# The norm of the group after next starts one front earlier: an SSM mixer stack on one core

## The chip, the cores and the metric

The kernel runs on one core of a Trainium2 chip. The metric is the device time of one execution in microseconds, over several runs. Everything is computed in float32 (a few masks and sums in 16 bits), from inputs in HBM to an output in HBM.

## The reference, cut to what matters

The input is x, four sequences of 1024 tokens with 512 features. Four layers run one after the other: a Mamba-2 mixer A, a gated feed-forward, a second mixer B, and the same kind of feed-forward again; each adds to the stream of tokens. A mixer is, cut to its core:

```
h    = layernorm(x)
z, hBC, dt = split(h @ in_proj)              # 1024, 1024 + 2*N, heads
hBC  = silu(causal_conv1d(hBC, taps=4))      # each channel by itself
h, B, C = split(hBC)
dt   = softplus(dt + dt_bias);  a = -exp(A_log) * dt
# in chunks: inside of a chunk and through a state S of each head
L    = exp(segment_sum(a))                   # lower triangle, per head
y    = ((C B^T) * L) @ (dt * h)  +  exp(cumsum a) * (C S)  +  D * h
S    = exp(sum a) * S + B^T (decay * dt * h)
y    = gated rms norm of y and silu(z)       # A: gate, then norm; B: norm, then gate
x    = x + y @ out_proj
```

Mixer A has 16 heads of 64 channels and a state of 64, mixer B 64 heads of 16 channels and a state of 128. A feed-forward normalizes x, forms a gate from a 512 x 512 product, an aggregate with a 512-2048-512 network of one token per sequence, and a last norm.

## The kernel before, in words

**Tiles and stages.** The 4096 tokens are 32 tiles of 128. The stream x goes through HBM between the layers: each layer loads its tiles and stores them again. Mixer A takes the time from 0 to about 1145 us, the first feed-forward to about 1340, mixer B to about 2815, the last feed-forward to the end. The first feed-forward leaves its last twelve tiles unfinished; their last steps (`last_step`, L1367 to L1384: adds on POOL, a norm and two products on VectorE) run inside the norm of mixer B's groups.

**A mixer's groups.** A mixer works in 16 groups of two chunks (`GC = 2`), a chunk being one tile; four groups make a sequence. `Group` loads the two x tiles of a group (from the pool `xp`) on SP's queue. Three things happen to a group, in three different iterations of the main loop (L1005 to L1028). In iteration n, the chunks of group n run (`chunk`, L763 to L976). Between their yields the *front* of group n+1 is emitted piece by piece (`front`, L443 to L629). Inside that front the *norm* of group n+2 is emitted, again piece by piece (`norm`, L389 to L441).

**The norm** has three parts. *Measure*: statistics of both tiles on VectorE (L396 to L398) and a reciprocal root on POOL (L223). *Scaling*: one small VectorE operation for each tile (L417) and one ScalarE operation (L419) that writes the normalized tile xn. *Turning*: eight 128 x 128 transposes on TensorE (L434) into the tile xnT, with a ScalarE copy from PSUM for each token tile (L436); the first three columns of xnT are the previous group's last tokens, copied by POOL (L429). A group with unfinished tiles has its last steps ahead of measure, and measures each tile as soon as it is finished. The norm is a generator: without steps, its first `next` emits measure, the third the scaling, the sixth hands the transposes over; with steps the work is spread over nine.

**The front** has 18 pieces (17 in A): a *gate* piece is one 128-column part of the z product and, for every second, its tanh and the VectorE product L541; a *conv* piece is one product of in_proj (L347), the first tap on ScalarE (L470), three more on VectorE (L474), and the silu of the piece before (L481 to L494). The products for dt (L503, read on VectorE at L511) are small ones. The softplus of dt (from L548) is emitted beside the pieces from the seventh on.

**The order.** TensorE, VectorE, ScalarE and POOL execute exactly in the order of emission (`manual_schedule`); only SP's order (loads and small stores) is laid by the scheduler. Small products (dt, transposes, the sums of the next chunk: `prologue`) stand in a list `small`; each large product pops one after itself (L346), and `finish` empties what is needed at a chunk's beginning. A chunk yields an estimate of the time for which it would leave TensorE waiting; the main loop emits pieces of the front, at 1.75 or 1.9 us each, until that is used up. When the pieces are exhausted, the loop stops there and what is left in `small` goes at the next `finish`.

**A chunk of mixer B** has four quarters of the heads: `decays` forms the exponents of L in PSUM, ScalarE takes exp (L806), VectorE multiplies by C B^T (`weigh`, L813), and TensorE multiplies with the values (`inner`, L829) into py; `close_y` (L878 to L885), `to_state` (L909), and the tail of the chunk (`tail`: the output product L670, the sum of squares ssq L672, the update of x L686, its statistics L229) follow, the tail inside the next chunk. Mixer A has one quarter in each chunk.

**The last steps' buffers.** xp has six x tiles, xnT three buffers. A feed-forward loads its even tiles to five tiles of its own pool, its odd ones to six of xp.

Of the kernel before, what the change touches and what calls it, by code (L numbers as in the profile page):

```python
# [8 lines left out]
F32 = mybir.dt.float32  # L9
# [6 lines left out]
P = 128  # L16
GC = 2
GT = GC * P
D = 512
KD = D // P  # L20
# [5 lines left out]
HIST = TAPS - 1  # L26
# [46 lines left out]
def hybrid_kernel(  # L73
# [40 lines left out]
    NT = NB * NCH  # L114

    const = ctx.enter_context(tc.tile_pool(name="const", bufs=1))
    xp = ctx.enter_context(tc.tile_pool(name="xp", bufs=6, reuse_waits="tile"))
    dr = ctx.enter_context(tc.tile_pool(name="dr", bufs=1, space=bass.MemoryType.DRAM))
    wts = ctx.enter_context(tc.tile_pool(name="wts", bufs=1))

# [100 lines left out]
    def rsqrt(v):  # L221

        nc.gpsimd.tensor_tensor(v, v, neg_half[: v.shape[0]], ALU.pow)  # L223
# [23 lines left out]
    def mixer(m, in_w, conv_w, conv_b, dt_bias, A_log, Dv, norm_w, out_w, src, dst, first, stats, last_steps={}):  # L247
# [18 lines left out]
        with stack:  # L266
            wk = stack.enter_context(tc.tile_pool(name=f"wk_{m.name}", bufs=1, reuse_waits="tile"))
# [5 lines left out]
            def mm(name):  # L273
                return p_mm.tile([P, 512], F32, tag="mm", name=name)
# [69 lines left out]
            small = []  # L344
# [13 lines left out]
            def defer(part, steps, first=False):  # L358

                runs = []  # L360
                for n, step in enumerate(steps):
                    last = n == len(steps) - 1
                    if last:
                        pending.append((part, None))

                    def run(step=step, last=last):
                        step()
                        if last:
                            pending[:] = [p for p in pending if p[0] is not part]

                    runs.append(run)
                small[:] = runs + small if first else small + runs
# [16 lines left out]
            def norm(f, prev):  # L389

                tag = f.tag
                mv = sm.tile([P, GC, 3], F32, tag="mv_x", name=f"mv_{tag}")

                def measure(c):
                    st = sm.tile([P, 6], F32, tag="st_x", name=f"st_{tag}_{c}")
                    nc.vector.bn_stats(st, f.xs[c])  # L396
                    nc.vector.bn_aggr(mv[:, c, 0:2], st)
                    nc.vector.tensor_scalar_add(mv[:, c, 1:2], mv[:, c, 1:2], 1e-5)  # L398
                    rsqrt(mv[:, c, 1:2])

                if f.steps:

                    for n in range(6):
                        for c in reversed(range(GC)):
                            if 0 <= n - 2 * c < 4:
                                next(f.steps[c])
                            if n - 2 * c == 3:
                                measure(c)
                        yield
                else:  # L410
                    for c in range(GC):
                        measure(c)
                    yield
                    yield
                xns = []
                for c in range(GC):
                    nc.vector.scalar_tensor_tensor(mv[:, c, 2:3], mv[:, c, 0:1], -1.0, mv[:, c, 1:2], ALU.mult, ALU.mult)  # L417
                    xn = wk.tile([P, D], F32, tag="xn", name=f"xn_{tag}_{c}", bufs=2)
                    nc.scalar.activation(xn, f.xs[c], AF.Identity, bias=mv[:, c, 2:3], scale=mv[:, c, 1:2])  # L419
                    xns.append(xn)  # L420
                yield
                yield
                if not f.steps:
                    yield
                xnT = f.xnT = wk.tile([P, KD, HIST + GT], F32, tag="xnT", name=f"xnT_{tag}", bufs=3)
                if prev is None:
                    nc.gpsimd.memset(xnT[:, :, 0:HIST], 0.0)
                else:
                    nc.gpsimd.tensor_copy(xnT[:, :, 0:HIST], prev.xnT[:, :, GT : GT + HIST])  # L429

                def turn(c, k, tps={}):
                    if k == 0:
                        tps[c] = mm(f"tpx_{tag}_{c}")
                    nc.tensor.transpose(tps[c][:, k * P : (k + 1) * P], xns[c][:, k * P : (k + 1) * P], ident)  # L434
                    if k == KD - 1:
                        nc.scalar.copy(  # L436
                            xnT[:, :, HIST + c * P : HIST + (c + 1) * P], tps[c].rearrange("p (k t) -> p k t", k=KD)
                        )

                defer(xnT, [lambda c=c, k=k: turn(c, k) for c in range(GC) for k in range(KD)])  # L440
                yield  # L441

            def front(f, behind):  # L443
# [5 lines left out]
                tag = f.tag  # L449
                xnT = f.xnT  # L450
# [159 lines left out]
                more = norm(behind, f if behind.b == f.b else None) if behind is not None else iter(())  # L610
                soft = softplus()
                for at, (kind, n) in enumerate(steps):
                    if kind == "gate":
                        if n == 7:
                            defer(f, prologue(f, 0))
                        gate(n)
                        if n == 6:
                            silu(order[-1])
                    else:
                        convolve(order[n])  # L620
                        if n > 0:
                            silu(order[n - 1])

                    if at >= (2 if behind is not None and behind.steps else 4):
                        next(more, None)
                    if at >= 6:
                        next(soft, None)
                    yield 1.75 if kind == "gate" else 1.9
# [352 lines left out]
            with tc.manual_schedule(  # L981
                engines={
                    mybir.EngineType.PE,
                    mybir.EngineType.DVE,
                    mybir.EngineType.Activation,
                    mybir.EngineType.Pool,
                }
            ):
                fs = [Group(*groups[0]), Group(*groups[1])]
                for _ in norm(fs[0], None):  # L990
                    pass
                if first:
                    lay_constants()
                    lay_flags(range(TS))
                weighing = weigh_rows()
                for at, _ in enumerate(front(fs[0], fs[1])):
                    catch_up()
                    if at >= 6:
                        next(weighing, None)
                for _ in weighing:  # L1000
                    pass
                lay_sums(fs[0], 0)
                if first:
                    lay_flags(range(TS, SETS))
                for n in range(len(groups)):  # L1005
                    if n + 2 < len(groups):
                        fs.append(Group(*groups[n + 2]))
                    f, ahead, behind = (fs + [None, None])[n : n + 3]
                    pieces = front(ahead, behind) if ahead is not None else iter(())
                    due = 0.0  # L1010
                    for c in range(GC):
                        following = (f, c + 1) if c + 1 < GC else (None if ahead is None else (ahead, 0))
                        for us in chunk(f, c, following):
                            due += us
                            while due > 0.0:
                                waiting, later_on[:] = later_on[:], []
                                piece = next(pieces, None)
                                for step in waiting:
                                    step()
                                if piece is None:  # L1020
                                    break
                                due -= piece
                            catch_up()
                    for _ in pieces:
                        catch_up()
                state.pop("fold")()
                for _ in state["tail"]:
                    catch_up()  # L1028
# [3 lines left out]
    def ffn(r, src, dst, stats, filling, bias_on_pe):  # L1032
# [10 lines left out]
        with stack:  # L1043
            wk = stack.enter_context(tc.tile_pool(name=f"wk_f{r}", bufs=1, reuse_waits="tile"))
# [4 lines left out]
            p_c = stack.enter_context(tc.tile_pool(name=f"c_f{r}", bufs=2, space=PSUM))  # L1049

            def load_tile(i, name):
                pool, n = ((wk, 5), (xp, 6))[i % 2]
                t = pool.tile([P, D], F32, tag="x", name=name, bufs=n)
                nc.sync.dma_start(t, src[i])
                return t
# [94 lines left out]
            for s in range(4):  # L1150
                tag = f"{r}_{s}"
# [60 lines left out]
            for i in filling[: len(filling) - last]:  # L1212
                tag = f"{r}_{i}"
# [129 lines left out]
            behind = [] if leaves else [(i, True) for i in filling]  # L1343
# [123 lines left out]
```

## Time and profile before

| | us |
|---|---|
| median of 3 runs | 3059.65 |
| the 3 runs | 3053.1 to 3065.45 |
| profiled execution, its own time | 3044.65 |
| its span (first to last instruction) | 3042.9 |
| TensorE busy in the span | 2767.9 |
| VectorE busy | 2081.7 |
| ScalarE busy | 1261.8 |
| POOL busy | 720.3 |
| mean granted TensorE clock | 0.963 |

The profile is one execution, taken on the core. Its first page gives busy time by engine, then the costliest groups of instructions by line. Behind it the trace can be asked for the waits of each engine (which instruction waited for which, the total, how often, and the longest), for a table of busy time by stretches, and for the order of time of all instructions in a stretch, with the idle time of the engine before each and what ended it. Names have a letter for the layer: _a, _b for the mixers, _f for a feed-forward. PE is TensorE, PEld its weight loads, DVE VectorE, ACT ScalarE, POOL GpSimd, SP the engine whose queue issues the loads.

### The profile page before, as it was taken

Reading aid. Unit: us, or ns where it says so; the run is one execution under the profiler, and the core shown is the slowest. Engines: PE = TensorE matmul, PEld = TensorE weight load, DVE = VectorE, ACT = ScalarE, POOL = GpSimd, SP = SyncE. Lnnn points to the kernel's source line nnn. Section 1 sums busy time; section 2 is a strip of 40 time slices with the busy share of each in tenths; the row PEclk is TensorE's granted clock in tenths of the full one; section 3 lists DMA queues with packets and bytes.
Section 4 is the critical chain, followed back from the end, with each engine's and each line's share of the span. In section 5 each row is a group of like instructions: output and inputs, shape, how many; then the busy total and the mean of one; then the engine's idle time right before and its main releaser. Section 6 shows DMA issues by size and latency. Waiting matters only on the chain. (4 is left out here: it accounts for less than half of the span.)

```text
span 3042.9 us, 46127 instructions
## 1 busy us (share of the span) xinstructions
PE 2767.9 (91%) x17156; PEld 1789.5 (59%) x17156; DVE 2081.7 (68%) x4417; ACT 1261.8 (41%) x2874; POOL 720.3 (24%) x839
## 2 busy tenths in 40 slices
PE   7999999999999988999999899999888888898986
PEld 5666666666666653456666666666555565564332
DVE  5667666766666662477777687776787777875368
ACT  3334433334333332355444444444444444443245
POOL 1222122122212221351111112212222222212057
PEclk8999999999999999999999999999999999998999
DMA  3000000000000015430000000000000000001423
GB/s 117 14 19 16 16 16 17 24 17 17 16 17 22 10 68 205 154 102 10 17 20 20 13 20 18 13 17 21 22 25 21 20 23 20 13 11 72 170 88 110
DMA packets 92959, 124.25 MB, mean 41 GB/s; under 512 B 38728, under 2 KB 42328, under 8 KB 92736
## 3 DMA queue, kind: packets, MB, share of 16 engines
q1 hardware_dynamic: 80960, 98.23, 10.0%
q10 hardware_dynamic: 9792, 16.82, 1.5%
q0 software_dynamic: 1984, 6.26, 0.6%
q8 instruction: 136, 2.23, 0.3%
q14 instruction: 87, 0.71, 0.1%
HBM read 84.54 MB, written 36.72 MB: 40 GB/s over the span
## 5 line engine op out<-in xcount | busy, mean ns | idle before, releaser
L347 PE MATMUL pc_b<-xnT_b,w_in_b 128*128 128x259 f32 x1280 | 355.7, 408 | 25.1 <-DVE S_b L909 21.9
L813 DVE TENSOR_TENSOR L_b<-L_b,Gm_b 128x1024 f32<-128x1024 f32 x256 | 308.7, 1247 | 2.9 <-ACT L_b L806 2.9
L347 PE MATMUL pz_a<-xnT_a,w_in_a 128*128 128x256 f32 x1024 | 296.5, 408 | 2.9 <-ACT Bt_a L756 2.3
L347 PE MATMUL pc_a<-xnT_a,w_in_a 128*128 128x259 f32 x1152 | 299.1, 394 | 0.0
L806 ACT ACTIVATE L_b<-seg_b 128x512 f32<-128x512 f32 x512 | 263.6, 603 | 74.0 <-PE seg_b L799 74.0
L347 PE MATMUL pz_b<-xnT_b,w_in_b 128*128 128x256 f32 x1024 | 291.4, 397 | 2.9 <-ACT xnT_b L436 2.9
L474 DVE SCALAR_TENSOR_TENSOR u_b<-pc_b,cw_b,u_b 128x256 f32<-128x256 f32 x480 | 231.5, 482 | 79.8 <-ACT u_b L470 68.3
L347 PEld LDWEIGHTS pc_b<-xnT_b,w_in_b 128*128 128x128 f32 x1280 | 229.3, 198 | 92.7 <-DVE S_b L909 25.4
L474 DVE SCALAR_TENSOR_TENSOR u_a<-pc_a,cw_a,u_a 128x256 f32<-128x256 f32 x432 | 208.2, 482 | 73.6 <-ACT u_a L470 63.3
L1205 PE MATMUL g_ps<-gw,xnT_f 128*128 128x512 f32 x512 | 246.9, 619 | 9.6 <-DMA gw<-in_L_ffn_gate_w 4.2
L829 PE MATMUL py_b<-L_b,hdt_b 128*32 128x128 f32 x4096 | 165.7, 299 | 97.6 <-DVE L_b L813 96.5
L670 PE MATMUL pout_a<-w_out_a,h_a 128*128 128x512 f32 x512 | 240.2, 613 | 0.0
L670 PE MATMUL pout_b<-w_out_b,h_b 128*128 128x512 f32 x512 | 235.7, 604 | 0.0
L347 PEld LDWEIGHTS pc_a<-xnT_a,w_in_a 128*128 128x128 f32 x1152 | 200.9, 190 | 58.5 <-DVE rs_a L685 11.4
L882 POOL TENSOR_TENSOR h_b<-h_b,z_b 128x256 f32<-128x256 f32 x128 | 90.8, 730 | 509.5 <-ACT sq_b L881 509.5
L347 PEld LDWEIGHTS pz_a<-xnT_a,w_in_a 128*128 128x128 f32 x1024 | 172.3, 195 | 55.0 <-ACT out_a L679 14.4
L347 PEld LDWEIGHTS pz_b<-xnT_b,w_in_b 128*128 128x128 f32 x1024 | 174.5, 194 | 48.8 <-issue 26.0
L829 PEld LDWEIGHTS py_b<-L_b,hdt_b 128*32 128x32 f32 x4096 | 112.6, 117 | 147.7 <-DVE L_b L813 60.5
L1205 PEld LDWEIGHTS g_ps<-gw,xnT_f 128*128 128x128 f32 x512 | 93.2, 196 | 122.1 <-issue 113.5
L881 ACT ACTIVATE sq_b<-h_b 128x256 f32<-128x256 f32 x128 | 47.9, 417 | 262.5 <-DVE h_b L878 262.5
L670 PEld LDWEIGHTS pout_a<-w_out_a,h_a 128*128 128x128 f32 x512 | 93.3, 192 | 100.1 <-issue 96.3
L670 PEld LDWEIGHTS pout_b<-w_out_b,h_b 128*128 128x128 f32 x512 | 92.3, 190 | 99.5 <-issue 95.7
(321 smaller groups left out, 4919.7 us busy)
## 6 DMA issues: line engine op xcount, KB each, us to landing
d<-in_L_ffn_d_w SPq DMA_DIRECT2D x4, 2048.0 KB
x_f<-xa SPq DMA_DIRECT2D x32, 256.0 KB
xb<-x_b ACTq DMA_DIRECT2D x32, 256.0 KB
x_f<-xb SPq DMA_DIRECT2D x32, 256.0 KB
x_a<-in_L_attn_a_x SPq DMA_DIRECT2D x30, 256.0 KB
xa<-x_a ACTq DMA_DIRECT2D x30, 256.0 KB
out<-x_f SPq DMA_DIRECT2D x22, 256.0 KB
xf<-x_f SPq DMA_DIRECT2D x20, 256.0 KB
```

Source lines behind the costliest of these rows:

```text
L347: nc.tensor.matmul(*args, **kw)
L474: nc.vector.scalar_tensor_tensor(u, ps[:, k : k + GT], cw[:, j, k : k + 1], u, ALU.mult, ALU.add)
L670: nc.tensor.matmul(pout, f.hs[e // 2][:, e % 2, cols], w_out[:, e, :], **on)
L806: nc.scalar.activation(L[:, r], sg[r0 + r], AF.Exp)
L813: nc.vector.tensor_mul(Lr, Lr, Gm.unsqueeze(1).to_broadcast([P, 2 * HB, P]))
L829: nc.tensor.matmul(py[cg * CT : (cg + 1) * CT, e % 4, :], hdt[:, h // HC, u : u + HC, :], Ls[half][:, r, hq, :], start=not started[cg], st ...
L881: nc.scalar.activation(sr, yh, AF.Square)
L882: nc.gpsimd.tensor_mul(yh, yh, zs[half * 2 + r][:, :, cols])
L1205: nc.tensor.matmul(ps, xnT[:, k, :], gw[:, k, :], start=(k == 0), stop=(k == KD - 1 and not bias_on_pe))
```

## The change

Four things are changed.

1. In `front`, the norm of the next group but one takes its step ahead of a piece's products instead of behind them, and begins at the first piece instead of the fifth (the third, where the group has unfinished tiles). Without steps, measure is emitted ahead of gate 0 instead of behind gate 2, the scaling ahead of conv 0 instead of behind conv 2, and the transposes are handed over ahead of gate 3 instead of behind gate 4.
2. The pool of x tiles has eight buffers instead of six, the pool of turned tokens xnT two instead of three.
3. Where no pieces are left, the main loop emits one small product for each 0.35 us of the estimate instead of stopping.
4. A feed-forward's even tiles have four buffers of its own pool, its odd tiles the eight of xp.

```diff
-    xp = ctx.enter_context(tc.tile_pool(name="xp", bufs=6, reuse_waits="tile"))
+    xp = ctx.enter_context(tc.tile_pool(name="xp", bufs=8, reuse_waits="tile"))
...
-                xnT = f.xnT = wk.tile([P, KD, HIST + GT], F32, tag="xnT", name=f"xnT_{tag}", bufs=3)
+                xnT = f.xnT = wk.tile([P, KD, HIST + GT], F32, tag="xnT", name=f"xnT_{tag}", bufs=2)
...
                 for at, (kind, n) in enumerate(steps):
+
+                    next(more, None)
                     if kind == "gate":
...
                             silu(order[n - 1])
-
-                    if at >= (2 if behind is not None and behind.steps else 4):
-                        next(more, None)
                     if at >= 6:
                         next(soft, None)
...
                                 if piece is None:
+
+                                    if small:
+                                        small.pop(0)()
+                                        due -= 0.35
+                                        continue
                                     break
...
-                pool, n = ((wk, 5), (xp, 6))[i % 2]
+                pool, n = ((wk, 4), (xp, 8))[i % 2]
```

## The prediction

> **What bounds the kernel now.** I read the busy totals, then the waits by engine, then busy time by stage, then the timeline of single groups. Rows give start, duration, engine, line, operation; brackets give the idle time before it and its cause.
>
> ```profile
> PE 2767.9 (91%) x17156; PEld 1789.5 (59%) x17156; DVE 2081.7 (68%) x4417; ACT 1261.8 (41%) x2874; POOL 720.3 (24%) x839
> ...
> PE py_b L829 <- DVE L_b L813: 96.5, 71, 5.8
> PE tpg L1193 <- ACT xn_f L1186: 34.9, 12, 3.2
> PE ssq_a L672 <- DVE sq_a L972: 28.8, 14, 2.7
> PE pc_b L347 <- DVE S_b L909: 21.9, 12, 2.2
> ```
>
> TensorE does 2767.9 us of a 3042.9 us span, so the time is its work plus its waits. The largest are in mixer B, where py (L829) waits for VectorE's weighing L813: 96.5 us in 71 waits. Few of these are spare capacity: TensorE's order is written by hand, and what stands behind a waiting matmul waits too. The stages:
>
> ```profile
> 100.00:1100.00 1000.00, 962.15 (x5162) 653.13 (x5161) 677.14 (x1603) 382.65 (x955) 209.64 (x277) 0.98 0.06 17
> 1470.00:2030.00 560.00, 521.66 (x3954) 355.62 (x3955) 409.02 (x793) 250.77 (x585) 101.58 (x115) 0.98 0.06 18
> 2080.00:2650.00 570.00, 501.36 (x3717) 338.63 (x3715) 440.11 (x835) 249.09 (x571) 148.31 (x146) 0.95 0.07 20
> 2910.00:3030.00 120.00, 91.47 (x260) 43.30 (x258) 98.81 (x197) 66.79 (x110) 90.00 (x90) 0.96 0.34 114
> ```
>
> Columns: window, its length, busy PE, PEld, DVE, ACT, POOL, granted clock, DMA share, GB/s. Mixer A (row 1) is bound by TensorE, 96% busy. Mixer B without unfinished tiles (row 2) is at 93%; its groups that also finish tiles of the first feed-forward (row 3) at 88%, with DVE and POOL busier. The last feed-forward (row 4) is VectorE's.
>
> **Moving the norm.** It removes and adds no engine instruction in a steady group: bn_stats and its two followers (L396 to L398) twice, L417 twice, two ACT scalings (L419), eight transposes, two ACT copies only change places. Here is what they stand in front of, from one group of mixer B without steps:
>
> ```profile
> 1570.10 0.22 DVE L511 TENSOR_TENSOR v_b<-pd_b,dtb_b 128x64 f32<-128x64 f32 x1 [1.88 <-PE pd_b L503]
> ...
> 1572.72 0.22 DVE L511 TENSOR_TENSOR v_b<-pd_b,dtb_b 128x64 f32<-128x64 f32 x1 [2.33 <-PE pd_b L503]
> ...
> 1576.22 0.56 ACT L470 ACTIVATE u_b<-pc_b,cb_b,cw_b 128x256 f32<-128x256 f32 x1 [0.50 <-PE pc_b L347]
> ...
> 1578.12 1.51 DVE L474 SCALAR_TENSOR_TENSOR u_b<-pc_b,cw_b,u_b 128x256 f32<-128x256 f32 x3
> ...
> 1579.61 2.35 DVE L813 TENSOR_TENSOR L_b<-L_b,Gm_b 128x1024 f32<-128x1024 f32 x2
> ...
> 1582.02 0.65 PE L829 MATMUL py_b<-L_b,hdt_b 128*32 128x128 f32 x16 [0.37 <-DVE L_b L813]
> ...
> 1589.75 0.68 DVE L396 BATCH_NORM_STATS2 st_b<-x_b 128x6 f32<-128x512 f32 x1
> ...
> 1595.92 0.82 ACT L419 ACTIVATE xn_b<-x_b,mv_b 128x512 f32<-128x512 f32 x1 [1.69 <-DVE mv_b L417]
> ```
>
> *Measure.* It takes VectorE from 1589.75 to 1591.75, 2.0 us. Its new place is ahead of the first L511, where VectorE idles 1.88 and 2.33 us for TensorE: hidden, 0. At the old place nothing is gained: afterwards VectorE waits 0.94 us more for ACT's u (L470), which waits for products, before L813 of the last heads can come.
>
> *Scaling.* In the new order, L417 stands on VectorE after both first L813, rs, the x update and its statistics, just ahead of L474 at 1578.12; the two L419 stand on ACT directly ahead of the u (L470) that L474 reads, which was done at 1576.78. So u now waits for L417, which is ready at about 1578.2: two scalings at a pitch of 0.72 plus L470 at about 0.6 end near 1580.3. Add the semaphore and L474 starts near 1580.4, where it started at 1578.12: a VectorE bubble of about 2.2 us. Behind it stand L691 and the L813 that py at 1582.02 waits for already (0.37 us). Nothing is left to hide it, so TensorE stops 2.2 us longer. ACT's next four exponentials, behind u too, end near 1582.5 instead of 1580.8, ahead of their L813 at 1585. In the old order the same bubble was 1.69 us of ACT, ahead of nothing urgent.
>
> *Transposes.* Eight of 0.27 us, about 0.11 us each beyond what overlaps, 0.9 us, go from the second chunk to the first. In the second chunk TensorE has a 2.03 us wait for S (L909), which is VectorE's, and only grows by what is taken away. Their ACT copy (pitch 0.47) now stands ahead of a u in the first chunk: +0.48, less 0.14 for the L417 that left, +0.3; the order of the rest gives −0.2. Per group 2.2 + 0.3 − 0.2 = 2.3 to 2.4. Bounds: 1.5 if L417 is ready sooner, 3.5 if the copy is waited for in full. Eight groups: **+19** (12 to 28).
>
> *The clock.* A rule to weigh:
>
> ```profile
> 1543.00:1546.50 3.50, 1.47 (x10) 1.24 (x7) 3.46 (x7) 2.33 (x6) 1.42 (x2) 1.00 0.11 28
> 1546.50:1550.00 3.50, 3.50 (x39) 2.61 (x38) 2.50 (x7) 2.05 (x6) 0.00 (x0) 0.51 0.10 24
> ```
>
> One wait of 2.03 us lies in the first row; in the next 3.5 us the granted clock is 0.51. The Trainium skill ("TensorE: Matmul & The Clock Gate", section "HAM oscillation") sets the limit at idle gaps above about 3.4 us; by it a 2.2 us bubble costs 2.2. By the row it can cost another half of 3.4 us, 1.7. The row decides that it can happen; how often, no row says: I take three groups in ten, 8 × 0.3 × 1.7 = **+4** (0 to +14).
>
> **Groups with steps (six, mixer B).**
>
> ```profile
> 2302.94 3.43 DVE L813 TENSOR_TENSOR L_b<-L_b,Gm_b 128x1024 f32<-128x1024 f32 x2
> ...
> 2317.19 1.59 DVE L1384 SCALAR_TENSOR_TENSOR x_b<-sgl,mv_o,x_b 128x512 f32<-128x512 f32 x1
> ...
> 2323.66 2.35 DVE L813 TENSOR_TENSOR L_b<-L_b,Gm_b 128x1024 f32<-128x1024 f32 x2
> ```
>
> Their norm starts two pieces earlier. Now one tile's tail (L1383, L1384 and L396 to L398, 0.74 + 0.75 + 1.0 beside nothing on POOL, about 2.6 us with the pitch; 1.59 instead of 0.75 where POOL works) runs after the last L813 of the chunk (2323.66, for which TensorE waits 5.3 us); after the change both tiles' tails stand in front of it: +2.6. The xn bubble adds up to 2.1 to the first chunk. POOL's adds (1.8 to 2.2 us) fall beside earlier L813, where two took 3.43 instead of 2.35. The work earlier in VectorE's idle gives back 0.3 to 1.7 at ssq. I take +4.5 of 0 to 6: **+27** (0 to 36).
>
> **Mixer A.** There ssq's wait for L972 (2.2 us a group) sits where measure was behind; it vanishes, but the same scaling bubble, 2.2, lands on h (L878) and the next open of py: net 0, **−2** in all for the first group of each batch (range −10 to +10).
>
> **Starts.** In the first front, measure of the second group stood behind enough work that it waited only 9.0 us for x:
>
> ```profile
> 36.89 0.69 DVE L396 BATCH_NORM_STATS2 st_a<-x_a 128x6 f32<-128x512 f32 x1 [9.03 <-DMA x_a<-in_L_attn_a_x]
> ```
>
> It now stands ahead of v, z and every u of that front, and x still lands at 36.9, as other loads fill the queue until then. VectorE then runs from 44 to 60 almost without idle, so most of what waits is lost: **+5** (3 to 8). In mixer B x is there early, and TensorE waits 2.83 us at 1377.7 for the softplus chain (L579), in which measure stands now: **−2**.
>
> **Ends.** In the last group of each mixer no pieces remain, and 13 small products (about 2 us) move from the start of the second chunk into its predecessor's waits: **−4.5** for both (0 to −6). Elsewhere pieces run out only at a chunk's last yield: 0.
>
> **Buffers.** x with eight tiles lets each load start one group earlier at the same place of SP's queue; mixers show only one x wait worth naming, the one above: 0. xnT with two: the third was written after the first's last reader in order, no wait. The feed-forward's even tiles get four buffers, its odd ones eight. A tile is released about eight turns (31 us) after it is loaded, so some loads start late: **+1** (0 to +6); behind them on SP stand the other tile loads, and whoever normalizes them.
>
> **The sum:** 19 + 4 + 27 − 2 + 5 − 2 − 4.5 + 1 = **+47.5** on the profiled execution, 3044.65 (span 3042.9 and 1.75 around it), so 3092. The median of the three runs is 3059.65, 15 higher; I add the difference there: **3107**.
>
> **Rivals.**
> 1. *Faster: the two us of measure were what the weighing waited for.* If L417 is ready before the chunk's first L813 in practice, no bubble comes, and VectorE reaches the last L813 of each chunk 0 up to 2.3 us earlier: 8 × 2.3 + half of ssq_a's 28.8 + 6 × 1 + 4.5, less 5 at the start, is about −38: 3021. For it: the 96.5 us row. Against: ACT's order and the 0.94 us wait. It decides on whether u (L470) of the first convolution waits for L417: if not, this wins.
> 2. *The bubble moves, the total doesn't.* TensorE makes the 2.2 us up at the later wait of 2.31 us for the last L813 (1597.6), as that L813 waited on VectorE's backlog alone: +19 and +4 vanish, step groups come to 0: 5 − 2 − 2 − 4.5 + 1 = −2.5: 3057. Against: everything behind on TensorE, the products that feed the later u among it, shifts alike.
> 3. *Step groups even out:* their early work fits VectorE's idle, +27 becomes 0: 3080.
> 4. *The x loads of the feed-forward stall:* every even tile of 32 late by 1 us: +16 on top, 3123.
>
> **How the numbers follow.** Main 0.5, step groups even 0.22, stalls 0.08, the neutral one 0.08, faster 0.12. The bound for a difference is 0.5%, 15.3 us, about what a measurement of this kernel can tell: below 3044.4 is faster, to 3074.9 the same. Faster 0.12, same 0.08, slower 0.80. The likeliest's own range is 3075 to 3135; with the neutral one below and stalls above, 3050 to 3140.
>
> **What would show it.** Right: ACT's L419 in mixer B starting with an idle before it ended by L417 and followed by L470, L474 with an idle near 2.2 us ended by ACT's u in the first chunk; py's wait for L813 up from 96.5 to about 130; ssq_a's gone, py_a's (L860, on h) up; x_a's wait at the start above 9 us and at an earlier place. Group period in B 88.6 to 91, with steps 95 to 99. Wrong: those waits absent, or the last L813's wait shrunk by as much.

## The result

The changed kernel takes 3083.6 us (median of four runs, 3081.53 to 3090.09); the kernel before, 3056.38 us in its four. The ratio is 1.0088, with a 95% interval from 1.006 to 1.0117: slower, by 18 to 36 us. The forecast was 3107 with a range of 3050 to 3140, slower at 0.80. The direction and the range held; the loss is a little over half of the +47.5 that was summed. The profiled execution has a span of 3079.6 us, 36.7 above the one of before. One of the four runs of a kernel below (every step behind the products, the first front in the old order) took 3727.06 us at a granted clock of 0.685 and is left out of its figures.

**The totals and the waits.** First the busy line of the changed kernel's page, then TensorE's waits (total us, times, longest).

```profile
PE 2775.0 (90%) x17156; PEld 1793.8 (58%) x17156; DVE 2067.0 (67%) x4417; ACT 1262.8 (41%) x2874; POOL 709.6 (23%) x839
```

```profile
PE py_b L828 <- DVE L_b L812: 104.9, 87, 4.5
PE tpg L1197 <- ACT xn_f L1190: 35.2, 13, 3.2
PE py_a L859 <- DVE h_a L877: 34.0, 27, 4.6
PE pc_b L347 <- DVE S_b L908: 26.5, 12, 2.2
...
PE seg_b L788 <- DVE S_b L908: 8.4, 8, 2.3
PE tph_b L708 <- ACT L_b L805: 7.4, 7, 1.4
```

(The lines of the file have moved by one to four: L812 is the weighing that was L813, L877 was L878.) The wait of ssq for the sum of squares in mixer A, 28.8 us before, is gone from the list. In its place stand py_a for h (15.8 before, 34.0 now), more of py_b, and two waits of mixer B that were small before: for S at seg (the product that forms the exponents of L) and for ACT at tph (the transposes of h).

By stage (window, length, busy PE, PEld, DVE, ACT, POOL, granted clock, DMA share, GB/s), with windows moved along where the stage moved:

```profile
100.00:1100.00 1000.00, 967.33 (x5217) 660.16 (x5216) 677.97 (x1623) 392.05 (x980) 212.94 (x278) 0.99 0.06 17
1470.00:2030.00 560.00, 504.25 (x3814) 341.72 (x3813) 393.78 (x777) 240.29 (x561) 99.46 (x115) 0.98 0.06 17
2130.00:2700.00 570.00, 494.57 (x3619) 332.95 (x3620) 425.64 (x813) 239.06 (x548) 130.16 (x140) 0.93 0.06 19
2950.00:3070.00 120.00, 90.03 (x248) 42.16 (x248) 100.95 (x202) 67.30 (x111) 92.81 (x92) 0.94 0.34 110
```

In the same 1000 us of mixer A TensorE now gets through 5217 matmuls where it did 5162; in the 560 us of mixer B without steps, 3814 instead of 3954; with steps, 3619 in 570 us instead of 3717, at a clock of 0.93 instead of 0.95.

**Where the time went.** I cut both profiled executions at the first output product (L670) of each chunk. "Start" ends at the first of these; "steps" are the six groups of mixer B that finish tiles.

| stage | before, us | changed kernel |
|---|---|---|
| start | 94.0 | +9.0 |
| mixer A | 1051.2 | −19.0 |
| feed-forward 0 and start of mixer B | 282.1 | +3.0 |
| mixer B, eight groups without steps | 716.0 | +25.9 |
| mixer B, six groups with steps | 564.1 | +18.4 |
| last group of B | 98.4 | −2.0 |
| feed-forward 1 | 237.2 | +1.5 |

Two opposite effects are in the sum: mixer A is faster and mixer B slower, though the same code moves in both. The column is a difference of two single profiles; what it becomes over several is said behind the experiments.

**The place of the scaling.** The timeline of the changed kernel in a group's first chunk of mixer B, VectorE, ACT and TensorE in turn:

```profile
1481.96 0.22 DVE L417 SCALAR_TENSOR_TENSOR mv_b<-mv_b 128x1 f32<-128x1 f32 x2
1484.21 1.52 DVE L474 SCALAR_TENSOR_TENSOR u_b<-pc_b,cw_b,u_b 128x256 f32<-128x256 f32 x3 [2.03 <-ACT u_b L470]
...
1482.21 0.81 ACT L419 ACTIVATE xn_b<-x_b,mv_b 128x512 f32<-128x512 f32 x1 [2.65 <-DVE mv_b L417]
...
1482.93 0.80 ACT L419 ACTIVATE xn_b<-x_b,mv_b 128x512 f32<-128x512 f32 x1
1483.63 0.55 ACT L470 ACTIVATE u_b<-pc_b,cb_b,cw_b 128x256 f32<-128x256 f32 x1
...
1479.37 0.66 PE L347 MATMUL pc_b<-xnT_b,w_in_b 128*128 128x259 f32 x2
...
1484.71 0.33 PE L708 MATMUL tph_b<-ident,h_b 128*128 128x128 f32 x1 [1.00 <-ACT L_b L805]
...
1486.99 0.64 PE L828 MATMUL py_b<-L_b,hdt_b 128*32 128x128 f32 x16 [0.85 <-DVE L_b L812]
1488.13 0.65 PE L828 MATMUL py_b<-L_b,hdt_b 128*32 128x128 f32 x16 [0.49 <-DVE L_b L812]
...
1504.30 0.65 PE L828 MATMUL py_b<-L_b,hdt_b 128*32 128x128 f32 x16 [1.80 <-DVE L_b L812]
```

ACT stands idle 2.65 us for L417, although the product that u reads is finished (its last matmuls, L347, end at 1480.03). The two scalings and u follow, and VectorE waits 2.03 us for that u: the step that the prediction put at 2.2. TensorE pays 1.00 + 0.85 + 0.49 us where it paid 0.37. At the chunk's last weighing it gets 0.5 us back: 1.80 us, where it waited 2.31:

```profile
1509.30 0.64 PE L829 MATMUL py_b<-L_b,hdt_b 128*32 128x128 f32 x16 [2.31 <-DVE L_b L813]
```

(This line is the kernel before, in the same group.)

**Idle and clock together.** The trace also has the stretches of half clock. For the chunks of each kind I took their length, TensorE's idle (gaps over 0.15 us) and the time at half clock, all means in us. "First" and "second" are a group's two chunks, and in brackets stands how many were taken. Half of the half-clock time is lost, if TensorE has work: in the profile of before, successive products of mixer B at L347 start 221 ns apart at the full clock and 432 ns apart at the half one (medians).

| chunks | before: length, idle, half clock | changed | all steps behind the products (below) |
|---|---|---|---|
| A, first (13) | 33.73, 0.09, 0.00 | 36.70, 1.83, 0.79 | 35.16, 0.66, 0.00 |
| A, second (13) | 35.86, 2.63, 2.10 | 31.66, 0.48, 0.00 | 31.64, 0.48, 0.00 |
| B, first (8) | 46.55, 3.88, 2.56 | 50.76, 5.58, 5.12 | 47.29, 3.91, 1.28 |
| B, second (8) | 42.94, 3.02, 3.41 | 41.97, 4.21, 0.85 | 42.15, 4.12, 1.28 |
| B with steps, first (6) | 50.96, 6.23, 7.40 | 54.53, 8.54, 7.96 | 51.01, 5.84, 6.26 |
| B with steps, second (6) | 43.06, 4.12, 1.14 | 42.55, 3.43, 3.41 | 42.76, 3.59, 2.28 |

In a first chunk of B, +4.21 is 1.70 of idle, 1.28 of clock (half of 5.12 − 2.56) and a rest of 1.23, which I take for the transposes' work. In its second chunk 0.88 of work and 1.28 of clock go away, and 1.19 of idle comes.

### The profile page after: what moved, and what is told of

It is laid out like the page before. It is cut to its first block, busy times and chain, and to the rows that moved or that the text cites. A ratio compares the mean times of both kernels' runs of the same rounds, so it can differ in the third digit from the quotient of the medians.

```text
span 3079.6 us, 46072 instructions
## 1 busy us (share of the span) xinstructions
PE 2775.0 (90%) x17156; PEld 1793.8 (58%) x17156; DVE 2067.0 (67%) x4417; ACT 1262.8 (41%) x2874; POOL 709.6 (23%) x839
## 3 DMA queue, kind: packets, MB, share of 16 engines
q0 software_dynamic: 1984, 6.26, 0.6%
## 5 line engine op out<-in xcount | busy, mean ns | idle before, releaser
L347 PE MATMUL pc_b<-xnT_b,w_in_b 128*128 128x259 f32 x1280 | 366.6, 418 | 39.2 <-DVE S_b L908 26.5
L474 DVE SCALAR_TENSOR_TENSOR u_b<-pc_b,cw_b,u_b 128x256 f32<-128x256 f32 x480 | 231.7, 483 | 149.4 <-ACT u_b L470 138.0
L812 DVE TENSOR_TENSOR L_b<-L_b,Gm_b 128x1024 f32<-128x1024 f32 x256 | 308.4, 1246 | 2.8 <-ACT L_b L805 2.8
L347 PE MATMUL pc_a<-xnT_a,w_in_a 128*128 128x259 f32 x1152 | 306.2, 398 | 0.0
L347 PEld LDWEIGHTS pc_b<-xnT_b,w_in_b 128*128 128x128 f32 x1280 | 236.5, 203 | 109.8 <-DVE S_b L908 30.1
L347 PE MATMUL pz_a<-xnT_a,w_in_a 128*128 128x256 f32 x1024 | 295.3, 408 | 2.6 <-ACT Bt_a L755 1.9
L347 PE MATMUL pz_b<-xnT_b,w_in_b 128*128 128x256 f32 x1024 | 293.7, 398 | 3.1 <-ACT xnT_b L436 3.1
L474 DVE SCALAR_TENSOR_TENSOR u_a<-pc_a,cw_a,u_a 128x256 f32<-128x256 f32 x432 | 208.3, 482 | 91.8 <-ACT u_a L470 81.4
L828 PE MATMUL py_b<-L_b,hdt_b 128*32 128x128 f32 x4096 | 162.4, 292 | 106.1 <-DVE L_b L812 104.9
L347 PEld LDWEIGHTS pc_a<-xnT_a,w_in_a 128*128 128x128 f32 x1152 | 202.3, 193 | 60.0 <-DVE rs_a L684 11.4
L347 PEld LDWEIGHTS pz_b<-xnT_b,w_in_b 128*128 128x128 f32 x1024 | 174.5, 195 | 50.0 <-issue 25.0
L347 PEld LDWEIGHTS pz_a<-xnT_a,w_in_a 128*128 128x128 f32 x1024 | 172.4, 194 | 48.4 <-ACT out_a L678 19.7
L881 POOL TENSOR_TENSOR h_a<-h_a,z_a 128x256 f32<-128x256 f32 x128 | 93.1, 748 | 281.1 <-DVE h_a L877 250.7
```

The source lines that it names most:

```text
L347: nc.tensor.matmul(*args, **kw)
L474: nc.vector.scalar_tensor_tensor(u, ps[:, k : k + GT], cw[:, j, k : k + 1], u, ALU.mult, ALU.add)
L812: nc.vector.tensor_mul(Lr, Lr, Gm.unsqueeze(1).to_broadcast([P, 2 * HB, P]))
L828: nc.tensor.matmul(py[cg * CT : (cg + 1) * CT, e % 4, :], hdt[:, h // HC, u : u + HC, :], Ls[half][:, r, hq, :], start=not started[cg], st ...
L881: nc.gpsimd.tensor_mul(yh, yh, zs[half * 2 + r][:, :, cols])
```

## The experiments

My theory: the loss is the scaling's place ahead of a u on ACT. The rivals: the buffers; measure's own place on VectorE; the transposes in the first chunk; the half-clock stretches, by their phase alone. "Against before" and the ratios are medians against the runs of the kernel before on the same chip; stages are from the profiles.

**The buffers alone.**

```diff
-    xp = ctx.enter_context(tc.tile_pool(name="xp", bufs=6, reuse_waits="tile"))
+    xp = ctx.enter_context(tc.tile_pool(name="xp", bufs=8, reuse_waits="tile"))
...
-                xnT = f.xnT = wk.tile([P, KD, HIST + GT], F32, tag="xnT", name=f"xnT_{tag}", bufs=3)
+                xnT = f.xnT = wk.tile([P, KD, HIST + GT], F32, tag="xnT", name=f"xnT_{tag}", bufs=2)
...
-                pool, n = ((wk, 5), (xp, 6))[i % 2]
+                pool, n = ((wk, 4), (xp, 8))[i % 2]
```

> The kernel before with only the buffers changed: eight x tiles, two xnT, and four and eight tiles in the feed-forwards; no order of the hand-written engines changes. Theory (the cost is the norm's scaling that stands ahead of the first convolution's u on ACT): nothing moves in the mixers (each stage within 1.5 us of before), at most +2 in the feed-forwards, total 0 to +2. Rival (waits for x tiles or for xnT are the cost): +20 or more, in mixer B's groups, with DMA or POOL named as the releaser.

Measured: 3058.54 us, ratio 1.0001 (0.9986 to 1.0015). No stage moves by more than 2.5 us. The buffers cost nothing that these runs can tell.

**The small products alone.**

```diff
                                 if piece is None:
+
+                                    if small:
+                                        small.pop(0)()
+                                        due -= 0.35
+                                        continue
                                     break
```

> The kernel before with only the small products popped when the pieces are out. Theory: the last group of mixer A -2.5 and of mixer B -2, all other groups within 0.3 us each; total -4.5. Rival (mixer A's gain of 19 us in the changed kernel comes from these pops, not from measure's new place): mixer A -10 to -20 by itself.

Measured: 3055.27 us, ratio 0.9992 (0.9975 to 1.0009). In the profile the last group of A gains 2.7 us and that of B 2.0, as expected, and A's other groups keep their 2.6 us of idle; 4.5 us of 3056 is within the interval. Mixer A as a whole is 0.2 us longer, so these pops are not its gain. The same profile shows how large chance is: with the order of before everywhere else, its span is 3063.7 us, 21 longer. Its start alone is 7.4 us longer and has 30.7 us at half clock instead of 17.1; half of the difference is 6.8.

**All steps behind the products, still from the first piece on.**

```diff
                 for at, (kind, n) in enumerate(steps):
-
-                    next(more, None)
                     if kind == "gate":
...
                             silu(order[n - 1])
+                    next(more, None)
                     if at >= 6:
```

> The changed kernel, but each step of the norm stands behind the products of its piece, still from the first piece on: L417 and the scaling L419 now follow the u (L470) and the taps (L474) of the first convolution. Theory: the wait of L474 for u in mixer B's first chunks (2.0 us) and the py wait in mixer A (1.9 us) go; against the changed kernel -2 in each of 14 groups of B and -1.9 in 13 of A, some -45 in all if nothing takes their place, so 15 to 20 us faster than before, with the +9 at the start still there. Rival (the place of the half-rate clock windows and the transposes in the first chunk are the cost): mixer B's groups stay +2.5 to +3.5 each over before. Rival (the bubble only goes on to the second convolution's u): within 5 us of the changed kernel.

Measured: 3014.37 us, ratio 0.9849 (0.9821 to 0.9876), 69 us below the changed kernel. Its timeline at the same point:

```profile
1464.27 1.51 DVE L474 SCALAR_TENSOR_TENSOR u_b<-pc_b,cw_b,u_b 128x256 f32<-128x256 f32 x3
1465.70 0.22 DVE L417 SCALAR_TENSOR_TENSOR mv_b<-mv_b 128x1 f32<-128x1 f32 x2
...
1462.38 0.56 ACT L470 ACTIVATE u_b<-pc_b,cb_b,cw_b 128x256 f32<-128x256 f32 x1 [0.50 <-PE pc_b L347]
1465.94 0.82 ACT L419 ACTIVATE xn_b<-x_b,mv_b 128x512 f32<-128x512 f32 x1 [3.00 <-DVE mv_b L417]
```

L474 starts without a wait, as u is done 1.3 us before it; the scaling waits 3.00 us for L417 with nothing urgent behind it. More went than the bubbles: I had counted 45 us. Mixer B without steps is 0.5 us below before, with the transposes still in the first chunk, where the rival had it 2.5 to 3.5 us a group above. In the first chunks of B idle falls by 1.67 us and the half-clock time by 3.84 (1.92 lost); in A by 1.17 and 0.79. The bubble was paid about twice in B.

**Measure early, scaling and transposes in their old places.**

```diff
-                    next(more, None)
+                    if at < (6 if behind is not None and behind.steps else 1):
+                        next(more, None)
...
+                    if at >= (8 if behind is not None and behind.steps else 5):
+                        next(more, None)
```

> The changed kernel, but only measure (with the last steps) comes early; the scaling stands behind conv 2 and the transposes behind gate 4, where they stood before. Theory: no bubble in the first chunk; mixer B without steps within 1 us a group of before, mixer A 2 us a group below before as ssq no longer waits for L972 (-26), start +5 to +9, groups with steps +0 to +3 each; total -20 to 0 against before. Rival (measure's own new place costs, by what it delays on DVE): mixer B +2 or more a group here too.

Measured: 3038.46 us, ratio 0.9932 (0.9911 to 0.9954). Measure's new place is not the cost: idle in B's chunks is within 0.6 us of before, and the groups with steps are 0.3 us shorter each. Its clock stretches made B's first chunks 1.3 us longer all the same (half clock 5.12 instead of 2.56); the run with the small products alone, in B's old order, has 4.69 there, so profiles of one order differ by as much. In A I had been wrong about the wait of ssq: most of it does not go with measure.

```profile
PE ssq_a L674 <- DVE sq_a L974: 18.9, 14, 1.8
```

Mixer A is 23.7 us shorter, near the expected 26, but not by the vanishing of that wait. It was 28.8; measure holds 10 us of it. The rest is in the timeline of the kernel *before*, in a second chunk of A:

```profile
445.94 1.52 DVE L474 SCALAR_TENSOR_TENSOR u_a<-pc_a,cw_a,u_a 128x256 f32<-128x256 f32 x3 [2.26 <-ACT u_a L470]
...
443.32 1.52 ACT L419 ACTIVATE xn_a<-x_a,mv_a 128x512 f32<-128x512 f32 x2 [2.69 <-DVE mv_a L417]
444.75 0.71 ACT L885 ACTIVATE sq_a<-h_a 128x256 f32<-128x256 f32 x2
445.36 0.55 ACT L470 ACTIVATE u_a<-pc_a,cb_a,cw_a 128x256 f32<-128x256 f32 x1
```

The kernel before has the same bubble at the old place: scalings ahead of u (L470) on ACT, and VectorE waits 2.26 us for that u, with ssq's sum behind it. The change did not bring the bubble to A, it moved it.

**The scaling alone behind its piece's products.** Measure and transposes stay ahead, as in the changed kernel.

```diff
+                    scaling = 6 if behind is not None and behind.steps else 2
 
-                    next(more, None)
+                    if at != scaling:
+                        next(more, None)
...
+                    if at == scaling:
+                        next(more, None)
```

> The changed kernel with one step alone moved: the scaling (L417, L419) behind the products and taps of its piece (conv 0; conv 2 for groups with steps) instead of ahead of them; measure and the transposes stay ahead. Theory: the scaling's place ahead of u is the whole difference between the changed kernel and the one with all steps behind: within 8 us of 3014. Rival (transposes or measure ahead of the products cost as much): between 3040 and 3084.

Measured: 3020.19 us, ratio 0.9877 (0.9849 to 0.9904). One step moved by one piece's products gives 63 of the 69 us. Mixer A −46.4, B without steps +1.1 against before; only the groups with steps keep +8.0 (−1.4 with every step behind), presumably as there the last steps' VectorE work still stands ahead of the products; no run moves that work alone.

**The scaling written twice.** Each L419 runs twice with the same values.

```diff
                     nc.scalar.activation(xn, f.xs[c], AF.Identity, bias=mv[:, c, 2:3], scale=mv[:, c, 1:2])
+                    nc.scalar.activation(xn, f.xs[c], AF.Identity, bias=mv[:, c, 2:3], scale=mv[:, c, 1:2])
```

> The changed kernel with each of the two scalings L419 written twice (same values), so ACT has 1.44 us more at that place in every group. Theory: the bubble grows by about 1.4 us in each chunk it sits in: TensorE's idle +1.4 in 14 groups of mixer B and 13 of A, +38 against the changed kernel, and more than that if further half-clock windows follow the longer bubbles. Rival (ACT has slack there, and the loss lies in transposes, measure or clock): under +10.

Measured: 3155.23 us, ratio 1.0323 (1.0296 to 1.0349), 72 us above the changed kernel. The waits of VectorE and TensorE:

```profile
DVE u_b L475 <- ACT u_b L471: 165.5, 73, 4.5
...
DVE u_a L475 <- ACT u_a L471: 114.9, 61, 3.7
```

```profile
PE py_b L829 <- DVE L_b L813: 110.4, 72, 6.5
PE py_a L860 <- DVE h_a L878: 50.8, 27, 4.6
```

The waits for u, 138.0 and 81.4 in the changed kernel, grow by 27.5 and 33.5. ACT has no slack there: A's first chunks have 1.52 us more idle (1.44 was added) and 2.89 us more half clock, 1.45 lost; together 2.97, and the chunks are 2.82 longer. Over mixer A and the 14 groups of mixer B TensorE's idle grows by 37 us, as expected, and its time at half clock by 75, of which half is lost. In this kernel the price of a bubble is the bubble and about as much again by the clock; in the groups with steps the second part is smaller (9.0 us of idle, 3.4 of clock).

**The first front of each mixer in the old order.**

```diff
-                    next(more, None)
+                    if f is not fs[0]:
+                        next(more, None)
...
+                    if f is fs[0] and at >= 4:
+                        next(more, None)
```

> The changed kernel with the first front alone in the old order (measure behind gate 2 and so on); everything else is as in the changed kernel. Theory: VectorE's wait for x at the start falls from 21.6 us back to 9, TensorE's idle before the transposes from 11.6 to 7, and the first output product comes 4 to 9 us earlier; total -5 to -9 against the changed kernel. Rival (the +9 at the start is a longer stretch at half clock that comes by chance): 0 in the median of several runs.

Measured: 3083.59 us, ratio 1.0093 (1.0061 to 1.0124), the same as the changed kernel, as the rival had it. The wait for x does fall, from 21.59 us to 6.08, and TensorE's before the transposes from 11.58 to 4.05. But the start is 9.6 us above before: its profile has 20.5 us of half clock from 68 us on. Alone this run does not tell the order from the clock, so I added the same edit to the kernel with all steps behind, and later ran both again.

```diff
+                    if f is not fs[0] or at >= 4:
+                        next(more, None)
```

> The kernel with the norm's steps behind the products from the first piece on, and the first front alone in the old order. Theory: keeps the 42 us of the norm behind the products and gives back 4 to 10 at the start: about 3005 to 3010, faster than both kernels. Rival (the start is chance): 3014 as without it.

Measured: 3005.85 us, ratio 0.9826 (0.9799 to 0.9852).

> The kernel with all steps behind the products once more, beside the one with the old first front, to tell whether the first front's order matters (5 rounds). Theory (the longer wait for x costs): 5 to 9 us slower than the other. Rival (chance of the clock at the start): within 3 us.

> All steps behind the products, the first front in the old order, 5 rounds. Theory: 3003 to 3009 and 5 to 9 under the one with the new first front. Rival: within 3 us of it.

Measured: 3012.05 us (0.9854, 0.9834 to 0.9875) with the new first front, 3009.1 (0.9849, 0.9827 to 0.9871) with the old. Over both pairs the means of eight runs each are 3012.4 and 3007.0. Seven profiles have the old order in the first front (the one of before among them), and their starts lie −0.8 to +9.6 us from before, mean 4.6; seven have measure early there, +8.5 to +14.4, mean 12.0. So the order costs about 7 us at the start in these profiles, with a scatter of up to 10 inside of one order. In the totals 3 and 8.5 us show between the kernels with all steps behind, and none between the two with the scaling ahead; how much it costs there stays open within 0 to 9.

**The groups with steps in the old order.**

```diff
-                    next(more, None)
+                    if behind is None or not behind.steps:
+                        next(more, None)
...
+                    if behind is not None and behind.steps and at >= 2:
+                        next(more, None)
```

> The changed kernel with the norm of the groups that finish tiles (mixer B, six of them) in the old order and place, the others as changed. Theory (the steps and the scaling ahead of the products cost there what the profile of the changed kernel shows, 18 us): -15 to -20 against the changed kernel, mixer B's groups with steps within 2 us of before, everything else as in the changed kernel. Rival (their loss is the clock's phase, handed on from the groups before): under -6.

Measured: 3057.73 us, ratio 1.0009 (0.9996 to 1.0022). The stage goes from +18.4 to −0.7; in the spans 20 us come back, in the medians 26, more than the stage holds in that profile (the changed kernel with the first front in the old order has +24.0 there). The loss of those groups is their own, not handed on by the clock.

**A mixture.** Groups without steps are as in the run with the scaling alone behind, groups with steps have every step behind, and the first front is in the old order.

```diff
+                    stepped = behind is not None and behind.steps
+                    early = f is not fs[0] and not stepped and at != 2
 
-                    next(more, None)
+                    if early:
+                        next(more, None)
...
+                    if not early and (f is not fs[0] or at >= 4):
+                        next(more, None)
```

> A mixture: groups without steps have measure and transposes ahead of the products and the scaling behind; groups with steps have every step behind; the first front is in the old order. Theory: takes the shorter of the two orders in each stage, some 4 to 8 us under the kernel with all steps behind and the old first front: about 3000. Rival (differences that small are the clock's chance): the same within 5 us.

Measured: 3001.16 us, ratio 0.9821 (0.98 to 0.9843), the fastest of all, 55 us below before; that it beats the one with all steps behind and the old front (3005.85 and 3009.1) is not certain from these intervals.

```profile
PE 2751.8 (92%) x17156; PEld 1779.1 (59%) x17156; DVE 2059.6 (69%) x4417; ACT 1258.5 (42%) x2874; POOL 716.8 (24%) x839
```

TensorE's busy time, with the same 17156 matmuls, is 23 us below the changed kernel, with less of it at half clock (158.9 us in all, 234.7 in the changed kernel).

## Why the prediction was right, and where its sizes were off

| step of the sum | predicted | measured, one profile of each | several profiles of each order |
|---|---|---|---|
| B without steps, order | +19 | +25.9 with the clock | +20.2 with the clock |
| clock in these groups | +4 | in the line above | in the line above |
| groups with steps | +27 | +18.4 | +20.0 |
| mixer A without its last group | −2 | −16.3 | −17.7 |
| start | +5 | +9.0 | +7.3 |
| B's start | −2 | 0 to +0.5 | |
| last groups | −4.5 | −2.7 and −2.0 | |
| buffers | +1 | 0 (ratio 1.0001) | |

The last column takes means. The old order stands in the profiles of before, of the buffers alone and of the small products alone; the new one in those of the changed kernel and of the runs that go back to the old order elsewhere (first front, groups with steps). At the start it is seven profiles against seven.

*Right.* The scaling: VectorE's bubble of 2.03 us for 2.2, at the place and with the chain that was named; moving that one step removes 63 of 69 us. Measure costs nothing at its new place in B: VectorE's wait at L511 there fell from 87.8 to 63.2 us. The transposes bring nothing where they leave: idle of 1.19 us takes their place. The last groups and the buffers came as summed. Of the signs that were named, py's wait for the weighing rose to 104.9 us only, not to 130, and the group's period in B is 92.7 us, above the 88.6 to 91 that were given; with steps it is 97.1, inside 95 to 99.

*B's start and the last feed-forward.* The profile has +3.0 and +1.5, but the run with the small products alone, whose orders and buffers there are those of before, has +2.6 and +1.6: before's profile was quick there. The gain of 2 us at B's start is a miss: the wait at the softplus chain fell from 2.83 to 1.83 us, and other waits took that, 13.1 us of idle from 1300 to 1430 us in both.

*B without steps* was 23 in sum and came to 25.9, or 20.2 over several profiles, but not as cut, and that the sum is close is in part luck. The bubble was sized well: 1.97 us where it stands (1.00 + 0.85 + 0.49, less 0.37). What failed is the term of the transposes. The prediction says that the second chunk gains nothing when they leave it, yet their 0.9 us in the first chunk are not in its 2.2 + 0.3 − 0.2. They came to 1.23 us of work there, and the last weighing's wait, for which the prediction allowed nothing, gave 0.5 back. The clock was put at +4. In this pair its terms cancel: first chunks have 2.56 us more at half clock, second chunks 2.56 less. Over three profiles of each order the stage has 19.3 us more idle, and its half-clock time is 4.5 us shorter. A net cost of the clock in this stage is not shown.

*Groups with steps.* The step that failed: "after the change both tiles' tails stand in front of it: +2.6", for the last weighing of a first chunk. There the waits shrank instead. In one such group of the changed kernel:

```profile
2242.76 0.74 DVE L1387 SCALAR_TENSOR_TENSOR sgl<-sgl,mv_o,gam 128x512 f32<-128x512 f32 x1
...
2248.85 1.52 DVE L474 SCALAR_TENSOR_TENSOR u_b<-pc_b,cw_b,u_b 128x256 f32<-128x256 f32 x3 [2.03 <-ACT u_b L470]
...
2252.36 0.64 PE L828 MATMUL py_b<-L_b,hdt_b 128*32 128x128 f32 x16 [2.36 <-DVE L_b L812]
```

The wait for the last weighing is 2.36 us, 4.10 in the same group before:

```profile
2229.97 1.08 PE L829 MATMUL py_b<-L_b,hdt_b 128*32 128x128 f32 x16 [4.10 <-DVE L_b L813]
```

It is shorter in five of the six groups. VectorE's work is paid earlier: as a mean of the six, py's waits come to 6.3 us (6.1 before), and 1.3 us are added in waits for S (2.35 us at seg in the group shown) and 0.8 in waits for hdt, the values times dt. Idle rises by 2.31 us in first chunks and falls by 0.69 in second ones, clock takes 1.42 more: 3.1 a group, not 4.5.

*Mixer A* is the large miss: −16 lies outside its own range of −10 to +10, and it made the forecast of the total too high. "The same scaling bubble, 2.2, lands on h (L878) and the next open of py: net 0" nearly holds for idle: −0.41 us a group, as second chunks lose 2.15 and first ones gain 1.74. The reason given for the wait of ssq was wrong, though: measure holds 10 us of its 28.8, the scaling at its old place the rest. What failed in the sum is that I priced both bubbles at their length. The wait of ssq was followed by half clock for 2.10 us a group, the new one for 0.79. Half of that difference, 0.65 a group, with the idle and 0.2 of work makes 1.23 in 13 groups: −16.0.

*The start.* TensorE's idle before the transposes grew by 4.6 us (7.00 before, 11.58 now), as summed; most of the rest goes with the half clock, 23.9 us of it for 17.1.

```profile
35.88 0.69 DVE L396 BATCH_NORM_STATS2 st_a<-x_a 128x6 f32<-128x512 f32 x1 [21.59 <-DMA x_a<-in_L_attn_a_x]
```

*From span to median.* The sum was made on a profiled execution of 3044.65, near the fast end of that kernel's runs (3045.77 to 3064.18 in all later ones); the changed kernel's, 3081.53, is 2 us below its median. So the spans differ by 37 us and the medians by 27. Adding a difference to a median was right; the difference of two single profiles carries some 10 us of chance, and the stage means of the last column agree with the medians.

*The rivals.* "Faster" was decided by whether u waits for L417. It does, and the run without that wait is 42 us faster than before: 3014 measured, 3021 given. That the figures are close is chance: the rival's gain was to come for the most part from mixer B, 18 us without steps and 6 with, and that run gains 0.5 and 1.4 there and 41.8 in mixer A. "The bubble moves" holds for the 0.5 us at the last weighing only. "Step groups even out" (3080) fits the total best, by accident: those groups lost 18 us, and mixer A gave back nearly as much.

## What to carry to other kernels

When a step is moved ahead on an in-order engine, look at what stands directly behind each of its instructions and on what they wait: here two ACT operations of 0.8 us, which nobody needed soon, held the one operation that VectorE and then TensorE waited for. Put work with slack behind the urgent instruction of the same stretch, not ahead of it. A TensorE bubble of about 2 us is not priced by its length alone; count the half clock behind it, and compare such kernels by several runs, stage by stage.

## What the hardware showed that I had not expected

The granted clock halves behind gaps well under the 3.4 us that the prediction weighed. In the changed kernel the first window has the chunk's waits for the weighing, the longest of 1.80 us:

```profile
1502.00:1505.70 3.70, 1.32 (x27) 0.67 (x29) 3.67 (x7) 1.07 (x3) 0.00 (x0) 1.00 0.00 0
1505.70:1509.10 3.40, 3.40 (x22) 2.54 (x15) 2.04 (x6) 0.75 (x2) 1.09 (x2) 0.50 0.00 0
```

TensorE was busy 1.32 of 3.70 us and then ran 3.4 us at 0.50. The half-clock stretches last 3.41 us or a multiple, up to 20.5 (a last one at the very end of a trace excepted), and from 150 us on they begin on one grid of 3.41 us through each of the fourteen profiles. I cut all fourteen on their grids and took the windows at full clock. Where TensorE was busy for under 0.40 of the window, half clock followed in all of 400; from 0.40 to 0.50, in 99 of 202; from 0.50 up, in 15 of 10444. Among windows whose longest gap was 1 to 2 us the busy share still decides: under 0.40, 72 of 72, and from 0.50 up, 8 of 442. So in these kernels a bubble costs half clock by what else TensorE waits for in the same window, more than by its own length.

In the changed kernel the stretches recur in B's first chunks at 1505.7, 1597.8, 1690.0, 1782.2, 1874.3, 1966.5 and 2058.6, that is every 92.2 us, 27 times 3.41; in the kernel before the commonest distance of those in second chunks is 88.7, 26 times. Whether the group's length settles on such multiples by itself, no run here was made to tell. And between the profile of before and that of the small products alone, 21 us apart with nearly the same order, the half-clock time differs by 33.4 us, which accounts for 16.7 of them.
